# Splitting the staged row tiles into thirds for a one-block convolution, with loads six units ahead

## The chip, the core and the metric

The kernel runs on one core of a Trainium2 chip. The metric is the device time of one execution in microseconds (us). Before the change three runs took 3682.8, 3675.8 and 3668.18 us; their median, 3675.8 us, is the time before. The profiled execution spans 3665.1 us from its first to its last instruction.

Names used below: PE is TensorE (PEld its weight loads), ACT is ScalarE, DVE is VectorE, POOL is GpSimd, SP is SyncE, whose queue (SPq in the profile) issues most of the DMAs.

## What is computed

Input x has shape (2, 256, 64, 64): B = 2 images, C = 256 channels, 64 rows of 64 pixels, all in float32. Layer 0 is full attention over the 4096 pixels of an image with 8 heads, then a 1x1 convolution and a blend with a mask. Layer 1 gates the channels, runs attention in 8x8 windows, adds that to its input, shuffles the channels in four groups, and ends with two grouped 7x7 convolutions whose sigmoid gates the result. The change concerns this last part, in the reference:

```python
x = x + o
g = 4
x = x.reshape(b, g, c // g, h, w).transpose(0, 2, 1, 3, 4).reshape(b, c, h, w)
y = lax.conv_general_dilated(x, sa_w1, (1, 1), [(3, 3), (3, 3)], feature_group_count=cr)  # 256 -> 64
y = relu(_bn(y + sa_b1, bn1...))
y = lax.conv_general_dilated(y, sa_w2, (1, 1), [(3, 3), (3, 3)], feature_group_count=cr)  # 64 -> 256
y = _bn(y + sa_b2, bn2...)
return x * sigmoid(y)
```

## The kernel before

**Main loop.** The function `pipeline` walks 1024 slots (image b, chunk c of 512 queries, group g of four heads, block m of 128 keys), in an order written out by hand (`tc.manual_schedule()`): the instructions of each engine run in the order in which the Python code emits them. Each slot has score matmuls on PE (L483), exponentials on ACT (L491), value products on PE (L505) and sums for the softmax denominators on DVE (L507). Beside these slots, `stage(b, c)` does what remains of layer 0 and the window attention of layer 1 for one chunk of eight image rows. Its last step writes the eight rows of `xo` to the DRAM scratch `x_s[b]` (L734, L739, the names xo and xs in the profile).

**The convolutions.** `convolve(b, blocks)` is a generator that is advanced a step at a time between slots. The 64 image rows are cut into three row blocks, `BLOCKS = ((0, 0, 24), (17, 24, 40), (34, 40, 64))`: first row loaded, first and last row of the result; 30 rows are loaded for each. The image b = 0 is convolved in one pass over all three blocks. The image b = 1 is convolved in two passes: blocks 0 and 1 as soon as chunk 5 is staged, and block 2 alone, `convolve(1, (2,))`, after the last chunk, when the attention slots are over and nothing else is left to run.

A pass works through `NU = 8` units of 32 channels (eight groups of four). For a unit u:

- `load_w(u)` (L760 to L764) loads the band matrices of both convolutions, w1 and w2, 896 KB each, from DRAM, into a pool of four buffers that both share (`wsp`).
- `load_x(u)` (L766 to L772) loads the unit's image rows from `x_s[b]`: for each row block four DMAs of 30 rows x 8 channels x 70 pixels, 65.6 KB. The destination is one of two fixed tiles `xcs[0]` and `xcs[1]`, each with room for three row blocks: `[P, len(BLOCKS), UG, WP]`.
- `conv1(u)` runs the first convolution as 112 matmuls (L782) from w1 and the x tile, and ACT writes the rectified result into `yc` (L790).
- `conv2(u)` runs the second as 112 matmuls (L803) from w2 and `yc` into two PSUM tiles; ACT turns these into the gate z by a tanh (L813) and a scale (L819).
- `gate(u, z)` multiplies z by the x tile on DVE (L825) and POOL issues the output DMAs (L832), four for each row block.

The x tile of a unit is thus read twice, by conv1 and, at the unit's very end, by gate.

**The order of a pass.** First load_w(0) and load_w(1); then load_x(0) and load_x(1); then conv1(0); and for each u: conv1(u+1), conv2(u), gate(u), then load_w(u+2) and load_x(u+2). PE therefore runs conv1(0), conv1(1), conv2(0), conv1(2), conv2(1), conv1(3) and so on, ending with conv2(6), conv2(7). SP issues in the same order: the two weight DMAs of a unit, then its row DMAs. A DMA whose buffer is not free, or whose source is not written yet, holds up the whole SP queue behind it. For the last pass, load_w(0) and load_w(1) are emitted early, at the start of the last stage (the list `ahead`). In the built program a weight DMA of unit u in the last pass waits for these readers of its buffer: w1 of unit u for conv2(u-3), w2 of unit u for conv1(u-1); for u = 2, w1 waits for conv1(0) and w2 for conv1(1). The DMAs of SP also use eight completion counters in turn, so each waits for the landing of the one eight places before it.

Of the kernel before, what the change touches and what calls it, by code (L numbers as in the profile page):

```python
# [17 lines left out]
B, C, H, W = 2, 256, 64, 64  # L18
# [16 lines left out]
KS, PAD = 7, 3  # L35
# [5 lines left out]
BLOCKS = ((0, 0, 24), (17, 24, 40), (34, 40, 64))  # L41
NG = C // 4
UG = 8
NU = NG // UG
# [8 lines left out]
def conv_seq_kernel(ctx: ExitStack, tc: tile.TileContext, a, out):  # L53
# [6 lines left out]
    def psum2(name):  # L60
        return ps.tile([P, 2, CH], F32, tag="s", name=name)
# [18 lines left out]
    xcs, ycs = [], []  # L80
# [41 lines left out]
    with (  # L122
# [19 lines left out]
        for b in range(B):  # L142
            src = a["x"][b].rearrange("(k p) h w -> p k (h w)", p=P)
            for c in range(NCHUNK):
                x = x0.tile([P, KC, CH], F32, tag="x", name=f"x0_{b}_{c}")
# [220 lines left out]
    for kc in range(KC):  # L366
        d = wf[:, kc, kc * P : (kc + 1) * P]
# [7 lines left out]
    def pipeline(arm, shifted, pools):  # L375
# [191 lines left out]
        def stage(b, c):  # L567
            x, f = xts.pop((b, c)), fts.pop((b, c))
            if (b, c) == (B - 1, NCHUNK - 1):

                assert not convs
                ahead.append(convolve(b, conv_after[b, c]))
                next(ahead[0])
# [171 lines left out]
            if (b, c) in conv_after:  # L745
                convs.append(ahead.pop(0) if ahead else convolve(b, conv_after[b, c]))
# [7 lines left out]
        def convolve(b, blocks):  # L754
            nb = len(blocks)
            xs, w1s, w2s, ys = {}, {}, {}, {}
            dst = out[b].rearrange("(g i) r w -> i r g w", i=4)
            tag = f"{arm}_{b}_{blocks[0]}"

            def load_w(u):  # L760
                for ws, d, i in ((w1s, w1_s, 1), (w2s, w2_s, 2)):
                    t = wsp.tile([P, 32, UW], F32, tag="w", name=f"w{i}{tag}_{u}")
                    nc.sync.dma_start(t, d[u])
                    ws[u] = t  # L764

            def load_x(u):  # L766
                x = xs[u] = xcs[u % 2]
                for n, blk in enumerate(blocks):
                    r = BLOCKS[blk][0]
                    for q in range(4):  # L770
                        gs = slice(NG * q + UG * u, NG * q + UG * u + UG)
                        nc.sync.dma_start(x[4 + q : 4 + 4 * RB : 4, n], x_s[b][r : r + RB, gs, :])  # L772

            def conv1(u):
                if u >= NU:
                    return
                x, w = xs[u], w1s.pop(u).rearrange("p m (g d) -> p g d m", g=UG)
                s = psum2(f"c1{tag}_{u}")
                for q in range(2):
                    for d in range(KS):  # L780
                        for j in range(4):
                            nc.tensor.matmul(  # L782
                                s[32 * j : 32 * j + 32, q, 0 : nb * W],
                                w[:, 4 * q + j, d, :],
                                x[:, 0:nb, 4 * q + j, d : d + W],
                                start=(d == 0),
                                stop=(d == KS - 1),
                            )
                y = ys[u] = ycs[u % 2]
                nc.scalar.activation(  # L790
                    y[:, :, 0:nb, PAD : PAD + W],
                    s[:, :, 0 : nb * W].rearrange("p q (n x) -> p q n x", n=nb),
                    AF.Relu,
                )

            def conv2(u):
                y, w = ys.pop(u), w2s.pop(u).rearrange("p m (i q d) -> p q d (m i)", q=2, i=4)
                tiles = [psum2(f"c2{tag}_{u}_{hh}") for hh in range(2)]
                for q in range(2):
                    for d in range(KS):  # L800
                        for j in range(4):
                            r = slice(32 * j, 32 * j + 32)
                            nc.tensor.matmul(  # L803
                                tiles[j // 2][:, j % 2, q * nb * W : (q + 1) * nb * W],
                                w[r, q, d],
                                y[r, q, 0:nb, d : d + W],
                                start=(d == 0),
                                stop=(d == KS - 1),
                            )
                z = cp.tile([P, 2, 4, len(BLOCKS) * W], F32, tag="z", name=f"z{tag}_{u}")  # L810
                z = z[:, :, :, 0 : nb * W]
                for hh in range(2):
                    nc.scalar.activation(  # L813
                        z[:, :, 2 * hh : 2 * hh + 2, :],
                        tiles[hh][:, :, 0 : 2 * nb * W].rearrange("p j (q f) -> p q j f", q=2),
                        AF.Tanh,
                        scale=0.5,
                    )
                nc.scalar.activation(z, z, AF.Copy, bias=0.5, scale=0.5)  # L819
                return z  # L820

            def gate(u, z):
                x = xs.pop(u)
                z = z.rearrange("p q j (n x) -> p (q j) n x", n=nb)
                nc.vector.tensor_mul(  # L825
                    z, z, x[:, 0:nb, :, PAD : PAD + W].rearrange("p n g x -> p g n x")
                )
                for n, blk in enumerate(blocks):
                    x0, r0, r1 = BLOCKS[blk]
                    for i in range(4):  # L830
                        p0, p1 = (4 * (r + 1 - x0) + i for r in (r0, r1))
                        nc.gpsimd.dma_start(  # L832
                            dst[i, r0:r1, UG * u : UG * u + UG, :], z[p0 : p1 - 3 : 4, :, n, :]
                        )

            load_w(0)
            load_w(1)
            yield
            load_x(0)
            load_x(1)  # L840
            yield
            conv1(0)
            yield
            for u in range(NU):
                conv1(u + 1)
                yield
                z = conv2(u)
                yield
                gate(u, z)
                if u + 2 < NU:  # L850
                    load_w(u + 2)
                    load_x(u + 2)
                yield

        def run_convs():
# [134 lines left out]
```

## Time and profile before

| What | Before |
|---|---|
| median time (three runs) | 3675.8 us |
| span of the profiled execution | 3665.1 us |
| PE busy over the span | 3382.0 us (92%) |
| DVE busy | 2718.2 us (74%) |
| ACT busy | 2328.0 us (64%) |
| last attention product (L505) ends | about 3454 us |
| last write of rows to x_s issued | 3520.37 us |
| last pass: first conv1 matmul | 3528.71 us |
| last pass: last conv2 matmul ends | 3655.28 us |
| last output DMAs issued | 3657.37 us to 3659.81 us |

Up to about 3454 us the attention slots keep PE, ACT and DVE busy together. From there to 3520 us the last stage runs alone, and then the last convolution pass alone. So the profile has to be read for that stretch by itself: the busy shares of the whole span say nothing of it. In the views used below, the chain of waits gives for each step its start, its length and what it was; the timeline gives for each merged row the start, the length, the engine, the line, the operation, and in brackets the idle time of the engine before it and what ended it; the view of stretches gives the busy time of each engine in each stretch with the granted TensorE clock (1.00 is full speed), the share in which the DMA engines were busy, and the bytes moved.

### The profile page before, as it was taken

What the parts mean: (1) busy time and instruction counts of PE and PEld (TensorE: products, weight loads), DVE (VectorE), ACT (ScalarE), POOL (GpSimd) and SP (SyncE); (2) the same over time, 40 slices, a digit from 0 to 9 for tenths busy, and PEclk for the clock granted to TensorE, in tenths of its full rate; (3) what the DMA queues carried; (4) which work ended last, traced back from release to release, by engine and by line L of the source; (5) the groups of instructions that cost most, each with busy time, mean ns of one, the idle gap of its engine ahead of it and who ended that gap; (6) DMA issues with size and microseconds to landing.
All of it is one profiled execution on the core that took longest, in us unless ns stands there. A gap on an engine that the chain in (4) does not pass through costs nothing.

```text
span 3665.1 us, 60054 instructions
## 1 busy us (share of the span) xinstructions
PE 3382.0 (92%) x25482; PEld 1223.8 (33%) x25482; DVE 2718.2 (74%) x1767; ACT 2328.0 (64%) x2549; POOL 231.4 (6%) x377
## 2 busy tenths in 40 slices
PE   9999999999999999999999899999999999779865
PEld 3432222222222222222234443323232323445345
DVE  3229989898989898989895565798989898545710
ACT  2238777777777777777775555677777777435510
POOL 5400000000000000000001111000000000011001
PEclk9999999999999999999999999999999999889965
DMA  8642112121212121112232232121212121332222
GB/s 311 191 132 64 52 52 59 51 60 50 62 47 62 49 62 50 53 56 55 61 114 90 86 108 79 50 62 51 61 49 60 49 61 50 117 116 88 69 79 92
DMA packets 139880, 284.86 MB, mean 78 GB/s; under 512 B 31560, under 2 KB 34012, under 8 KB 139600
## 3 DMA queue, kind: packets, MB, share of 16 engines
q1 hardware_dynamic: 120032, 242.60, 21.4%
q0 software_dynamic: 15760, 35.80, 3.6%
q8 instruction: 203, 3.33, 0.4%
q10 hardware_dynamic: 3808, 2.50, 0.2%
q14 instruction: 77, 0.63, 0.1%
HBM read 223.17 MB, written 60.65 MB: 77 GB/s over the span
## 4 chain that ended last, share of the span: by engine, by line
PE 41%; issue 27%; DVE 16%; ACT 3%; SPq 3%; DMA 3%; POOL 0%; DVEq 0%; ACTq 0%; POOLq 0%
PE sa L483 15%; PE ava L505 12%; DVE suma L507 11%; PE c2a L803 5%; PE c1a L782 3%; SPq L772 3%; PE qka L632 2%; ACT ea L491 2%; DMA xc<-xs 1%; DVE rda L528 1%; PE vwa L649 1%; PE opa L724 1%; DVE za L825 1%; PE hya L583 1%; PE ca1a L606 1%
## 5 line engine op out<-in xcount | busy, mean ns | idle before, releaser
L507 DVE TENSOR_TENSOR suma<-suma,ea 128x2048 f32<-128x2048 f32 x960 | 2199.7, 2291 | 448.9 <-ACT ea L491 371.2
L491 ACT ACTIVATE ea<-sa 128x1024 f32<-128x1024 f32 x2048 | 1984.5, 1023 | 428.7 <-PE sa L483 292.5
L483 PE MATMUL sa<-qa,ka 32*128 32x512 f32 x8192 | 1350.5, 650 | 72.6 <-ACT ea L491 40.3
L505 PE MATMUL ava<-ea,va 128*32 128x512 f32 x8192 | 1110.0, 614 | 0.0
L483 PEld LDWEIGHTS sa<-qa,ka 32*128 32x128 f32 x8192 | 436.0, 185 | 923.0 <-issue 479.6
L505 PEld LDWEIGHTS ava<-ea,va 128*32 128x32 f32 x8192 | 162.3, 108 | 795.7 <-issue 793.3
L782 PE MATMUL c1a<-xc,w1a 128*32 128x192 f32 (+2 forms) x2688 | 106.8, 336 | 124.6 <-DMA xc<-xs 124.6
L739 POOL DMA_DIRECT2D xs<-xo x32 | 28.4, 892 | 2397.4 <-DVE xo L734 2396.9
L803 PE MATMUL c2a<-yc,w2a 32*128 32x192 f32 (+2 forms) x2688 | 172.3, 415 | 1.0 <-issue 1.0
L803 PEld LDWEIGHTS c2a<-yc,w2a 32*128 32x128 f32 x2688 | 167.2, 336 | 15.6 <-issue 13.6
L832 POOL DMA_DIRECT2D out_dram<-za x192 | 112.5, 594 | 750.5 <-ACT ea L491 501.9
L632 PE MATMUL qka<-ua,qkv_w 128*128 128x512 f32 x256 | 128.5, 625 | 28.7 <-ACT qka L640 25.0
L782 PEld LDWEIGHTS c1a<-xc,w1a 128*32 128x32 f32 x2688 | 97.6, 156 | 143.1 <-issue 135.5
L790 ACT ACTIVATE yc<-c1a 128x384 f32<-128x384 f32 (+2 forms) x24 | 9.3, 388 | 208.1 <-PE c1a L782 208.1
L825 DVE TENSOR_TENSOR za<-za,xc 128x1536 f32<-128x1536 f32 (+2 forms) x24 | 29.3, 1222 | 131.5 <-ACT za L819 131.5
L813 ACT ACTIVATE za<-c2a 128x768 f32<-128x768 f32 (+2 forms) x48 | 26.3, 594 | 155.2 <-PE c2a L803 155.1
L640 ACT ACTIVATE qka<-qka,qkv_b 128x512 f32<-128x512 f32 x64 | 44.0, 687 | 107.7 <-PE qka L632 106.5
L528 DVE RECIPROCAL rda<-rda 128x512 f32<-128x512 f32 x32 | 107.1, 3346 | 2.8 <-ACT rda L525 2.8
L507 DVE TENSOR_TENSOR suma<-ea,ea 128x2048 f32<-128x2048 f32 x32 | 73.1, 2284 | 19.0 <-DMA ka<-ks 14.0
L632 PEld LDWEIGHTS qka<-ua,qkv_w 128*128 128x128 f32 x256 | 43.9, 191 | 113.5 <-issue 56.8
L724 PE MATMUL opa<-ota,out_w 128*128 128x512 f32 x128 | 65.3, 633 | 13.3 <-ACT ya L731 12.4
L166 DVE TENSOR_SCALAR qst<-q,bq 128x512 f32<-128x512 f32 x32 | 24.0, 751 | 69.3 <-PE q L155 45.0
(124 smaller groups left out, 1633.3 us busy)
## 6 DMA issues: line engine op xcount, KB each, us to landing
ka<-ks SPq DMA_DIRECT2D x256, 256.0 KB, 2.6
va<-vs SPq DMA_DIRECT2D x256, 256.0 KB, 2.6
w1a<-w1s SPq DMA_DIRECT2D x24, 896.0 KB, 4.7
w2a<-w2s SPq DMA_DIRECT2D x24, 896.0 KB, 6.6
xc<-xs SPq DMA_DIRECT2D x192, 65.6 KB, 2.5
xs<-xo POOLq DMA_DIRECT2D x32, 280.0 KB, 6.7
x<-in_x_dram SPq DMA_DIRECT2D x16, 512.0 KB, 4.9
ks<-kst SPq DMA_DIRECT2D x32, 256.0 KB, 2.5
```

Of the source, the lines that this page charges most:

```text
L483: nc.tensor.matmul(o, k[r, cols], q[r, g, :], start=True, stop=not shifted)
L491: nc.scalar.activation(e[:, 2 * hh : 2 * hh + 2, :], tiles[hh], AF.Exp, scale=SCALE0)
L505: nc.tensor.matmul(av[r, :], v[:, m % PB, r], e[:, j, :], start=start, stop=stop)
L507: nc.vector.tensor_add(total, first[0] if m == 1 else total, e)
L528: nc.vector.reciprocal(rd, rd)
L632: nc.tensor.matmul(s[:, j, :], wqkv[:, kc, o : o + P], u[:, kc, :], start=(kc == 0), stop=(kc == KC - 1),)
L724: nc.tensor.matmul(s[:, oc, :], wo[:, kc, oc * P : (oc + 1) * P], ot[:, kc, :], start=(kc == 0), stop=(kc == KC - 1),)
L772: nc.sync.dma_start(x[4 + q : 4 + 4 * RB : 4, n], x_s[b][r : r + RB, gs, :])
L782: nc.tensor.matmul(s[32 * j : 32 * j + 32, q, 0 : nb * W], w[:, 4 * q + j, d, :], x[:, 0:nb, 4 * q + j, d : d + W], start=(d == 0), stop=( ...
L803: nc.tensor.matmul(tiles[j // 2][:, j % 2, q * nb * W : (q + 1) * nb * W], w[r, q, d], y[r, q, 0:nb, d : d + W], start=(d == 0), stop=(d = ...
L825: nc.vector.tensor_mul(z, z, x[:, 0:nb, :, PAD : PAD + W].rearrange("p n g x -> p g n x"))
L832: nc.gpsimd.dma_start(dst[i, r0:r1, UG * u : UG * u + UG, :], z[p0 : p1 - 3 : 4, :, n, :])
```

## The change

A pass over nb row blocks now cuts each of the two x tiles into `len(BLOCKS) // nb` parts of nb row blocks, and unit u uses tile u % 2 and, within it, part u // 2 modulo the number of parts. For nb = 3 and nb = 2 there is one part, and everything is as before. For nb = 1, the last pass, there are three parts in each tile, so that six units have places of their own. `depth` is the number of places: 2 for the first two passes, 6 for the last. The rows of the first `depth` units are loaded before conv1(0), and after gate(u) the rows of unit u + depth go into the place that gate(u) has just read. It is meant to take the row loads off the path from one unit's gate to the next conv1. No instruction is added or removed; 24 row DMAs now stand together at the start of the last pass, where eight stood, and only those of units 6 and 7 are left between the weight DMAs.

```diff
             def load_x(u):
-                x = xs[u] = xcs[u % 2]
+                if u >= NU:
+                    return
+                n = u // 2 % (len(BLOCKS) // nb) * nb
+                x = xs[u] = xcs[u % 2][:, n : n + nb]
                 for n, blk in enumerate(blocks):
...
                             nc.tensor.matmul(
                                 s[32 * j : 32 * j + 32, q, 0 : nb * W],
                                 w[:, 4 * q + j, d, :],
-                                x[:, 0:nb, 4 * q + j, d : d + W],
+                                x[:, :, 4 * q + j, d : d + W],
...
                 nc.vector.tensor_mul(
-                    z, z, x[:, 0:nb, :, PAD : PAD + W].rearrange("p n g x -> p g n x")
+                    z, z, x[:, :, :, PAD : PAD + W].rearrange("p n g x -> p g n x")
                 )
...
             load_w(0)
             load_w(1)
             yield
-            load_x(0)
-            load_x(1)
+
+            depth = 2 * (len(BLOCKS) // nb)
+            for u in range(depth):
+                load_x(u)
             yield
             conv1(0)
...
                 gate(u, z)
                 if u + 2 < NU:
                     load_w(u + 2)
-                    load_x(u + 2)
+                load_x(u + depth)
                 yield
```

## The prediction

> **What bounds the kernel now.** The page first: PE is busy 92% of the span, yet its groups of instructions name one wait that has nothing to do with attention.
>
> ```profile
> L782 PE MATMUL c1a<-xc,w1a 128*32 128x192 f32 (+2 forms) x2688 | 106.8, 336 | 124.6 <-DMA xc<-xs 124.6
> L803 PE MATMUL c2a<-yc,w2a 32*128 32x192 f32 (+2 forms) x2688 | 172.3, 415 | 1.0 <-issue 1.0
> ```
>
> PE stood idle 124.6 us before first-convolution matmuls, always until rows had landed. The change touches only the last pass, so the next view is the waits of the stretch 3522 to 3665 us (us in total, times, longest):
>
> ```profile
> PE c1a L782 <- DMA xc<-xs: 53.7, 8, 10.1
> SPq L772 <- DVE za L825: 53.8, 6, 10.1
> ```
>
> The first line has eight waits; units 0 and 1 account for 10.09 and 0.51 us (their rows can't be read before the last stage has written them). The second says why the other six come late: SP holds the row loads of a unit until DVE has gated the unit two before. The chain of waits gives one such round whole (start, length, what):
>
> ```profile
> 3561.77 0.71 DVE za L825
> 3562.48 0.02 issue
> 3562.49 0.81 SPq L772
> 3563.31 0.05 issue
> 3563.36 0.77 SPq L772
> 3564.12 0.04 issue
> 3564.17 0.76 SPq L772
> 3564.93 0.04 issue
> 3564.97 2.42 DMA xc<-xs
> 3567.39 0.14 issue
> 3567.53 3.08 PE c1a L782 x112
> 3570.61 7.03 PE c2a L803 x112
> ```
>
> Gate, four DMA issues one after the other, a landing, conv1, conv2, and again. From the start of one conv1 to the next are 17.4 us, of which PE works 10.25. The idle times before conv1(2) to conv1(7) in the timeline are 6.90, 7.14, 7.53, 7.25, 7.13 and 7.19: together 43.1 us. That is all that the change can take.
>
> **How long the two convolutions take without the wait.** The view of stretches shows conv1(1), conv2 of a middle unit, and the end, where conv2(6) and conv2(7) stand together (PE, PEld, DVE, ACT, POOL busy; granted clock; DMA share; GB/s):
>
> ```profile
> 3532.00:3534.50 2.50, 2.06 (x116) 2.02 (x116) 0.00 (x0) 0.27 (x1) 0.00 (x0) 0.84 0.58 166
> 3623.30:3630.30 7.00, 6.98 (x112) 6.79 (x112) 0.00 (x0) 0.28 (x1) 0.00 (x0) 0.50 0.40 133
> 3640.70:3648.00 7.30, 7.30 (x116) 7.30 (x116) 0.00 (x0) 0.53 (x2) 0.00 (x0) 0.73 0.01 2
> 3648.00:3655.30 7.30, 7.26 (x110) 6.89 (x108) 0.69 (x1) 1.42 (x4) 2.44 (x4) 0.50 0.14 33
> ```
>
> conv2 takes 7.0 us at clock 0.50 and at 0.73: its weight loads, 6.79 us of 7.00, pace it. conv1 does depend on the clock: 2.08 us for conv1(1), warm behind conv1(0), and 3.22 at 0.50.
>
> **What the Trainium skill says.** "TensorE: Matmul & The Clock Gate", Part 1: the array runs at half clock until it has been busy through a free-running window of some 3.4 us, and falls back after an idle one. The trace agrees on the two levels, and goes further: between 3646 and 3655 us PE works without a break, in conv2 alone, and the clock is 0.50 all the same. So conv2 does not keep it up. The same page, "LDWEIGHTS", says that a weight load costs by its columns, not by its rows; conv2's loads (32 rows x 128 columns) take 6.90 us for 112 where conv1's (128 x 32) take 3.01, which agrees in direction. "DMA: Bandwidth & Descriptors", "Issuing engines are not separate DMA queues": all queues share 16 engines. And "Queues, rings and completion order" there: in a ring descriptors are taken in order, so rows issued behind weights wait for these. The trace has it for image 0, where the longest row landing is 10.3 us against a median of 2.4, at a DMA share near 1.
>
> **The change part by part.**
>
> *The row loads of units 2 to 5 go ahead: six waits on gates become two.* The built program shows no wait of their own on them but the landing of the eighth DMA before. At 0.81 us an issue, eight issues are 6.5 us, and a row landing is 2.5: no stall. Gone are the gaps before conv1(2) to conv1(5) as far as rows made them. Units 6 and 7 still wait for gate(0) and gate(1), but have 30 us and more before they are used: nothing.
>
> *What moves on SP.* In the trace the eighth row issue begins at 3529.52 and ends near 3530.3. Sixteen more at 0.81 take 13.0 us, to 3543.3. The weights of unit 2 stand behind them; w1 went out at 3531.99 before and now goes at 3543.3. Queued behind it on SP are w2(2), rows 6, w1(3); on PE conv1(2) and everything after wait for w1(2). It lands after 4.6 us (median of six w1 loads here), plus 0.15 to the first matmul: conv1(2) starts at S = 3548.05, where before it was 3550.15. So the first gap does not vanish; it shrinks by only 2.1 us, and its cause is now a weight load. A bound from the other side: in image 0's pass 24 row issues took 24.16 us, 1.0 each, under crowded DMA; at that rate S is 3551.2, a loss of 1.0 instead.
>
> *Units 3 to 7.* PE then runs conv1 3.22 and conv2 7.03, 10.25 a unit, if weights keep up:
> - w1(3) is free after conv2(0), issued behind rows 6 at about 3548.4, landed 3553.0; needed at S + 10.25 = 3558.3.
> - w2(3) waits for conv1(2), 3551.3; landed by 3556, needed much later.
> - Rows 7 wait for gate(1), which ends 2.1 us after conv2(1), at 3560.4; four issues to 3563.7; then w1(4), landed at 3568.3. Needed at S + 20.5 = 3568.55. Just in time; with 5.0, the longest landing here, 0.2 us late.
> - From then on no rows stand in the way: w1(u) goes when conv2(u-3) ends and has 10.25 us for 4.6. w2(u) goes when conv1(u-1) ends, some 20 us ahead.
>
> Five units at 10.25 are 51.25; from conv1(7) on the trace has 3637.47 to 3655.28, 17.81. I add 0.3 for w1(4) and seams: PE ends at 3548.05 + 51.25 + 17.81 + 0.3 = 3617.4, against 3655.28. The gain is 37.9 us: 2.1 from the first gap, 36.2 from the other five, less the 0.3. The tail behind conv2(7) stays.
>
> *The rest costs nothing.* Slices of the tiles change addresses, not instructions; the other two passes have one part and the same order. ACT, DVE and POOL work 1.57, 0.69 and 2.44 us a unit and lie beside 10.25 of PE. PSUM and the z buffers come free as before, behind a conv1 of 3.2 us. DMA bytes a unit: 1.84 MB of weights, 0.2 of output, in 10.25 us 198 GB/s; the trace shows 359 GB/s at full share in 3534.5 to 3537.1. There PE also lost 1.02 us inside conv2(0), while two weight loads stood together. That may recur where w1(4) and w2(4) follow each other; the trace doesn't show what it was, so I price it at nought to one us, take nought, and keep the rest for the range.
>
> **Rivals.**
> - *The clock rises.* Without gaps conv1 might run at 2.08: six times 1.14 is 6.8 less, 3631. Against it: the clock falls during conv2, as shown, and a conv2 stands before each of these conv1s.
> - *Weights take the place of rows in every unit.* If each w1 went out only as the PE became free for it, the gap would be 4.75 in place of 7.2: 5 x 2.45 + 2.1 = 14.4 saved, 3661. Against it: the buffers' waits as listed give w1 ten us of lead.
> - *DMA as the bound, slower than before.* If the DMA gave no more than the stretch's mean of 107 GB/s, 2.04 MB a unit would take 19.1 us, 1.65 more than now: five units 8.2, and 1.0 for the late S: 3685. For it: 24.16 us for 24 issues, a sign of crowding; against it: 359 GB/s moved in this same stretch.
>
> **How the numbers follow.** 3675.8 - 37.9 = 3637.9, rounded to 3638: chance 0.80. The clock 0.10, weights 0.06, DMA 0.04. The low end takes in the clock's 3631 and 6 for the spread of the runs before (3668.18 to 3682.8): 3625. The high end takes S at 3551.2 (+3.1), five stalls of 1 us, 0.5 more for w1(4) and 5.4 for that spread: 3652. Left out are weights and DMA, 0.10. Over 0.5% is 18.4 us: the first two cases are faster, 0.90; weights fall within 0.5%, with DMA mostly, 0.08; slower by more 0.02.
>
> **What would show it.** Right: after conv1(2), first-convolution matmuls without idle time on rows; conv1 starts 10.25 apart; one gap of about 5 us before conv1(2), ended by w1; SP issuing 24 row DMAs to about 3543; conv2(7) ending near 3617; clock 0.50 at each conv1. Wrong: a gap before every conv1 that ends with w1a; conv1 at 2.1 us; matmuls stretched or broken while weights move; rows landing late behind weights; another time before 3522.

## The result, and the profile after

The changed kernel takes 3633.02 us (median of four runs, 3626.75 to 3640.51) against 3671.99 us of the kernel before (four runs, 3665.8 to 3682.8): ratio 0.9892, 95% interval 0.9859 to 0.9924. Forecast were 3638 us within 3625 to 3652, and faster. Direction, size and place of the gain came as forecast; one term, the gap before conv1(2), did not. With four runs each, the interval allows a gain of about 28 to 52 us.

The page's two groups of the convolutions, which answer to those shown of before (L782 has become L785, L803 has become L806):

```profile
L785 PE MATMUL c1a<-xc,w1a 128*32 128x192 f32 (+2 forms) x2688 | 110.1, 342 | 92.3 <-DMA xc<-xs 73.5
L806 PE MATMUL c2a<-yc,w2a 32*128 32x192 f32 (+2 forms) x2688 | 172.1, 412 | 0.0
```

The idle time before first-convolution matmuls fell from 124.6 to 92.3 us, 32.3 less. The waits of the stretch from 3500 us to the end (us in total, times, longest) show what is left in the last pass:

```profile
PE c1a L785 <- DMA xc<-xs: 10.7, 2, 10.2
PE c1a L785 <- issue: 8.2, 2, 7.8
```

Rows are waited for twice, by units 0 and 1, as before. The other six waits of PE on rows are gone. In their place stand two that the profile puts down to nothing ("issue"). The SP queue's own waits say what SP was doing:

```profile
SPq L763 <- PE c2a L806: 17.0, 3, 6.8
SPq L763 <- PE c1a L785: 11.9, 4, 3.3
SPq L775 <- DVE za L828: 8.7, 1, 8.7
```

53.8 us in six waits of row loads on the gate have become 8.7 in one (rows 7 on gate(1)). The weight loads now wait for their buffers in good time. The chain of waits, from gate(0) to the start of conv1(4) (start, length, what):

```profile
3541.94 0.64 ACT za L822
3542.58 6.75 issue
3549.34 3.22 PE c1a L785 x112
3552.56 7.02 PE c2a L806 x111
3559.58 3.15 PE c1a L785 x112
3562.73 7.02 PE c2a L806 x110
3569.75 0.36 issue
3570.11 3.22 PE c1a L785 x112
```

Before the change a gate, four issues and a landing stood between one conv2 and the next conv1. Now conv1(3) follows conv2(1) at once, and so do all later ones but conv1(4), which is 0.36 us late. Only the gap before conv1(2) is still there. SP's timeline tells its cause (start, length, what):

```profile
3521.56 22.46 SPq L775 DMA_DIRECT2D xc<-xs  x24
3544.12 0.49 SPq L763 DMA_DIRECT2D w1a<-w1s  x1
3544.72 0.38 SPq L763 DMA_DIRECT2D w2a<-w2s  x1
```

w1(2) leaves SP behind 24 row issues and lands 5.1 us later, at 3549.2; conv1(2) starts at 3549.34. Last, the stretches that hold conv1(1), a conv2 in the middle, conv2(6) and conv2(7) (PE, PEld, DVE, ACT, POOL busy; clock; DMA share; GB/s):

```profile
3531.90:3534.20 2.30, 2.29 (x116) 2.23 (x116) 0.00 (x0) 0.00 (x0) 0.00 (x0) 0.82 0.40 86
3583.60:3590.60 7.00, 7.00 (x116) 6.90 (x112) 0.00 (x0) 0.28 (x1) 1.73 (x3) 0.74 0.61 208
3604.00:3611.30 7.30, 7.30 (x118) 7.30 (x116) 0.00 (x0) 0.52 (x2) 1.69 (x3) 0.73 0.12 29
3611.30:3618.60 7.30, 7.28 (x110) 6.91 (x110) 0.69 (x1) 1.43 (x4) 2.44 (x4) 0.50 0.15 33
```

conv2 keeps its 7.0 us with the DMA at 208 GB/s beside it, half as much again as the 133 of before.

**A length that can be compared.** The runs of one kernel spread over 14 us and more (up to 28 us in the experiments below), and the traces show where: the second write of rows to xs, which opens the last pass, is issued anywhere from 3515.93 to 3531.17 us, in a part of the program that the edits below leave as it is. So the experiments are read by the length of the last pass, from the issue of that second write to the end of conv2(7). Before it is 3520.37 to 3655.28, 134.9 us; after, 3519.74 to 3618.58, 98.8 us: 36.1 us less, by itself nearly the whole difference of the medians (39.0).

### The profile page after: what moved, and what is told of

Its sections match the earlier page's. It is cut to its first block, busy times and chain, and to the rows that moved or that the text cites. A ratio compares the mean times of both kernels' runs of the same rounds, so it can differ in the third digit from the quotient of the medians.

```text
span 3628.9 us, 60051 instructions
## 1 busy us (share of the span) xinstructions
PE 3372.7 (93%) x25482; PEld 1225.3 (34%) x25482; DVE 2718.9 (75%) x1767; ACT 2326.7 (64%) x2549; POOL 231.4 (6%) x377
## 3 DMA queue, kind: packets, MB, share of 16 engines
q8 instruction: 203, 3.33, 0.4%
## 5 line engine op out<-in xcount | busy, mean ns | idle before, releaser
L785 PE MATMUL c1a<-xc,w1a 128*32 128x192 f32 (+2 forms) x2688 | 110.1, 342 | 92.3 <-DMA xc<-xs 73.5
L806 PE MATMUL c2a<-yc,w2a 32*128 32x192 f32 (+2 forms) x2688 | 172.1, 412 | 0.0
L806 PEld LDWEIGHTS c2a<-yc,w2a 32*128 32x128 f32 x2688 | 167.1, 336 | 14.6 <-issue 12.7
L785 PEld LDWEIGHTS c1a<-xc,w1a 128*32 128x32 f32 x2688 | 99.4, 157 | 111.9 <-issue 101.5
## 6 DMA issues: line engine op xcount, KB each, us to landing
xc<-xs SPq DMA_DIRECT2D x192, 65.6 KB, 2.6
```

The source lines that it names most:

```text
L785: nc.tensor.matmul(s[32 * j : 32 * j + 32, q, 0 : nb * W], w[:, 4 * q + j, d, :], x[:, :, 4 * q + j, d : d + W], start=(d == 0), stop=(d = ...
L806: nc.tensor.matmul(tiles[j // 2][:, j % 2, q * nb * W : (q + 1) * nb * W], w[r, q, d], y[r, q, 0:nb, d : d + W], start=(d == 0), stop=(d = ...
```

## Experiments

Each kernel starts from the changed one. The table gives the length of the last pass and the idle time of PE in it from conv2(0) on. A gap stands before a convolution, and the number in brackets is that of the conv1 that waited; a break stands inside one. Each ratio is to runs of the kernel before made beside it.

| Kernel | Last pass, us | Idle, us | Median, us | Ratio to before (95%) |
|---|---|---|---|---|
| before | 134.9 | 43.1 in six gaps, break of 1.02 | 3672.0 | 1 |
| the change | 98.8 | gap (2) 7.84, (4) 0.36 | 3633.0 | 0.9892 (0.9859 to 0.9924) |
| the change again | 99.9 | gap (2) 9.23, (4) 0.73 | 3631.2 | 0.9899 (0.9874 to 0.9924) |
| own places, two ahead | 94.4 | gap (4) 1.48, (6) 0.94, (7) 0.40, break of 0.28 | 3638.3 | 0.9911 (0.9892 to 0.9930) |
| four ahead | 93.2 | gap (2) 3.25 | 3635.6 | 0.9901 (0.9882 to 0.9919) |
| weights of unit 2 first | 95.7 | gap (3) 4.00, break of 1.23 | 3630.4 | 0.9896 (0.9872 to 0.9919) |
| extra traffic | 103.7 | gap (2) 9.43, (4) 3.56, break of 0.66 | 3646.4 | 0.9921 (0.9898 to 0.9944) |
| three ahead | 90.6 | break of 1.20 | 3629.8 | 0.9894 (0.9867 to 0.9922) |
| three ahead again | 89.4 | none | 3625.4, one run | |
| pairs | 93.6 | breaks of 0.18, 1.40, 1.76 | 3625.7 | 0.9876 (0.9852 to 0.9901) |
| pairs again | 93.3 | breaks of 1.04, 0.89, 1.49 | 3622.2, one run | |
| pairs, weights left out | 88.4 | break of 0.45 | 3621.5, one run | |

The intervals of the ratios overlap: between the changed kernels only the last pass can be told apart, and it repeats within 1.2 us where it was taken twice (the change, three ahead, pairs).

### How far the last pass repeats

The changed kernel once more, with no edit, on the chip on which three ahead and the pairs first ran:

> The change itself once more, on the chip of the two runs beside it, for a direct comparison and as a measure of how far the length of the last pass repeats: 98.9 us from the second write of xs to the end of conv2(7), within 1 us if differences of 2 us between kernels are to be read; the gap before conv1(2) 7 to 9 us, that before conv1(4) below 1 us.

PE's timeline, conv1(2) and conv1(4):

```profile
3547.19 3.22 PE L785 MATMUL c1a<-xc,w1a 128*32 128x64 f32 x112 [9.23 <-issue]
...
3568.34 3.22 PE L785 MATMUL c1a<-xc,w1a 128*32 128x64 f32 x112 [0.73 <-ACT za L816]
```

The same two gaps, 1.4 and 0.4 us longer, and a last pass of 99.9 us against 98.8. Differences of some 2 us between the last passes of two kernels can therefore be read; smaller ones, as between two ahead and four ahead below, can not.

### Is it the place or the look-ahead?

```diff
-            depth = 2 * (len(BLOCKS) // nb)
+            depth = 2
```

> Edit: the thirds stay, but the rows are loaded two units ahead in the old order (rows 0 and 1 first, rows u+2 after gate(u) and behind the weights of u+2). Theory A, the wait was for the place that the gate still read: rows u+2 now wait only for SP to reach them, which is when w2(u+2) has gone out at the end of conv1(u+1). From there 0.35 + three issues of 0.81 + a landing of 2.7 = 5.5 us, or up to 7.8 if they ride behind w2, against 7.03 of conv2(u): gaps before conv1(2) to conv1(7) of 0 to 0.9 us, and w1(2) goes at 3532 again, so that the first gap is gone as well. PE would end 5 to 8 us before that of the change: 3625 to 3628 us, ratio to before 0.987 to 0.988. Theory B, it is the six units of look-ahead that matter, because rows are slow behind weights: gaps of 3 us or more before every conv1, 3648 us or more, ratio 0.993 or more.

PE's timeline in this kernel, the first convolutions of units 2 to 7 (the bracket is idle time before it):

```profile
3546.41 3.22 PE L785 MATMUL c1a<-xc,w1a 128*32 128x64 f32 x112
...
3556.71 3.22 PE L785 MATMUL c1a<-xc,w1a 128*32 128x64 f32 x112
...
3568.42 3.22 PE L785 MATMUL c1a<-xc,w1a 128*32 128x64 f32 x112 [1.48 <-ACT za L822]
...
3578.60 3.22 PE L785 MATMUL c1a<-xc,w1a 128*32 128x64 f32 x112
...
3589.78 3.04 PE L785 MATMUL c1a<-xc,w1a 128*32 128x64 f32 x112 [0.94 <-DMA xc<-xs]
...
3600.24 2.95 PE L785 MATMUL c1a<-xc,w1a 128*32 128x64 f32 x112 [0.40 <-DMA xc<-xs]
```

Three gaps of 2.8 us together are left of 43.1, with the row loads in the very order and as few units ahead as before. So the wait was for the place, theory A. Look-ahead adds little: rows that follow their own w2 through the queue land after up to 7.5 us, which is the odd microsecond late. That holds for the gap of 1.48 too, which is longer than the 0.9 allowed for: the profile names ACT, but the last rows of unit 4 land at 3568.3, just before conv1(4) starts. And the first gap is gone, because w1(2) is again the ninth DMA of the pass and not the twenty-fifth. The last pass is 4.4 us shorter than with six ahead, as theory A had it (5 to 8). The whole time does not show that. Its median, 3638.3, misses the 3625 to 3628 expected, and its interval (0.9892 to 0.9930) can't be told from that of the change: the runs are spread as said, and in the profiled one the pass began 3.6 us later than in that of the change.

### The first gap: how many row issues stand before w1(2)

```diff
-            depth = 2 * (len(BLOCKS) // nb)
+            depth = 2 if nb > 1 else 4
```

> Edit: rows of four units in place of six before the first conv1 of the last pass, then four ahead. Theory A, the gap before conv1(2) is w1(2) standing behind row issues on SP: eight issues fewer are 6.5 us, w1(2) goes at about 3537.5, lands by 3542.5, the gap falls from 7.8 to 1.0 to 1.5 us, and the 0.36 us before conv1(4) is gone, since no rows wait for a gate: about 3626 us, ratio 0.9875. Theory B, w1(2) is slow because weights and rows share the DMA engines: the gap stays above 5 us, 3631 to 3633 us.

SP, and conv1(2) on PE, in this kernel's timelines:

```profile
3545.36 0.50 SPq L763 DMA_DIRECT2D w1a<-w1s  x1
3545.96 1.09 SPq L763 DMA_DIRECT2D w2a<-w2s  x1
```

```profile
3553.01 3.22 PE L785 MATMUL c1a<-xc,w1a 128*32 128x64 f32 x112 [3.25 <-issue]
```

The eight issues fewer bring w1(2) forward from 24.4 to 16.9 us after the second write, 7.5 us, a little over the 6.5 expected. The gap before conv1(4) is gone too, since rows 6 and 7 no longer wait for a gate. But w1(2) landed after 7.6 us, 2.5 more than in the first trace of the change, so that 3.25 us of the gap are left in place of the 1.0 to 1.5 expected. The queue position, theory A, is the larger part. Theory B would put the long landing down to sharing: between 3544 and 3554 us the core's DMA moved 2.49 MB at 249 GB/s, of which w1(2) is 0.92. That is not shown. w2(2) goes out 0.6 us behind w1(2) here, but it does so in the two traces of the change and in the one with extra traffic as well, where w1(2) landed after 5.1, 6.2 and 4.7 us.

The other way to bring w1(2) forward is to let the weights of unit 2 go before the rows of units 2 to 5:

```diff
-            for u in range(depth):
+            for u in range(2):
                 load_x(u)
...
                 conv1(u + 1)
+                if u == 0 and nb == 1:
+                    load_w(2)
+                    for n in range(2, depth):
+                        load_x(n)
                 yield
...
-                if u + 2 < NU:
+                if u + 2 < NU and (u > 0 or nb > 1):
                     load_w(u + 2)
```

> Edit: six places and the loads six ahead, but the weights of unit 2 go out before the rows of units 2 to 5. Theory A: w1(2) goes at 3531.5, w2(2) at 3534.2, both land before conv2(0) ends at 3541.2; rows 2 behind them land by about 3541. The gap of 7.8 us before conv1(2) goes to 0 to 1 us, the 0.36 us before conv1(4) stays: 3625 to 3626 us, ratio 0.987. Theory B, rows and weights in the DMA engines are the limit: rows 2 come late instead, the gap is 3 us or more and the time 3628 us or more.

The first gap went, as theory A expected, but another came that neither theory named. On PE:

```profile
3540.65 3.22 PE L785 MATMUL c1a<-xc,w1a 128*32 128x64 f32 x112
3543.80 7.09 PE L806 MATMUL c2a<-yc,w2a 32*128 32x64 f32 x112
3554.89 3.22 PE L785 MATMUL c1a<-xc,w1a 128*32 128x64 f32 x112 [4.00 <-issue]
```

and on SP:

```profile
3532.21 17.41 SPq L775 DMA_DIRECT2D xc<-xs  x20
3549.72 0.49 SPq L763 DMA_DIRECT2D w1a<-w1s  x1
```

The twenty row issues, 17.4 us, now stand in front of w1(3). It lands 5.1 us after 3549.72 and conv1(3) starts at once. The burst of row issues has to be paid by whichever weights come next. Moved by one unit, it costs 4.0 us in place of 7.8: counted from the second write, w1(3) leaves 7.6 us later than w1(2) did in the change, but PE is ready for it 11.4 us later.

### Is the DMA near its bound?

```diff
+    w3_s = dram.tile([NU, P, 32, UW], F32, name="w3s")
...
                 conv1(u + 1)
+                if nb == 1 and u + 2 < NU:
+                    nc.scalar.dma_start(w3_s[u], w1_s[u])
                 yield
```

> Edit: the change, and beside it ACT issues one copy of a 917 KB weight block from DRAM to DRAM for each of units 2 to 7 (bytes that nothing reads), half as much again as the weights of a unit. Theory A, PE bounds the last pass and the DMA has room: w1(2) and w1(4) land 1 to 3 us later, the other units are unmoved at 10.2 us: 3634 to 3638 us, ratio 0.990 to 0.991. Theory B, the DMA is about to become the bound: a gap of 3 us or more before each conv1, 3651 us or more, ratio 0.994 or more.

```profile
3561.53 3.22 PE L786 MATMUL c1a<-xc,w1a 128*32 128x64 f32 x112 [9.43 <-issue]
...
3585.50 3.22 PE L786 MATMUL c1a<-xc,w1a 128*32 128x64 f32 x112 [3.56 <-DMA w1a<-w1s]
```

```profile
3573.88 5.81 SPq L776 DMA_DIRECT2D xc<-xs  x4
```

Half as much again of weight traffic lengthens the pass by 4.9 us over the first trace of the change and by 3.8 over the second. What is clear of their spread is one place: conv1(4), which waits 3.56 us against 0.36 and 0.73. Most of that is SP: the four issues of rows 7, which stand before w1(4), took 5.81 us, where they took 3.50 and 3.64 in the change. conv1(2) started 30.4 us after the second write, against 29.6 and 30.5 in the change, so the longer gap before it is not shown to come from the traffic. Units 3, 5, 6 and 7 follow without a gap; there is a break of 0.66 us inside conv1(7). So theory B, a gap of 3 us or more before each conv1, is out. The whole time, 3646.4, lies above the 3634 to 3638 that theory A gave; in the profiled run the pass began 11.4 us later than with the change, which is the larger part of it.

### The shortest pass

```diff
-            depth = 2 * (len(BLOCKS) // nb)
+            depth = 2 if nb > 1 else 3
```

> Edit: the thirds stay; rows of three units before the first conv1, then three ahead. Theory A, two queues have to be served at once: rows need only their own place and a unit of lead, and weights must not stand behind many row issues. w1(2) then goes 3.2 us later than with two units ahead, 3.5 us before it would be late; rows are landed before their conv1: no gap above 0.5 us before conv1(2) to conv1(7). From the second write of xs to the end of conv2(7) 91 to 92 us, against 98.9 for the change, 94.4 with two ahead and 93.2 with four. About 7 us below the change: ratio to before 0.987 to 0.989. Theory B, two weight loads together starve whatever else is loading: gaps of 1 us or more remain, 93 us or more.

> Three ahead once more, for a second trace of the shortest pass: 90 to 92 us from the second write of xs to the end of conv2(7), no gap ended by rows or by w1 above 0.5 us; a break of about 1 us inside a convolution may or may not come again.

The first trace has no gap ended by rows or weights, but a break inside conv1(2):

```profile
3536.96 1.72 PE L785 MATMUL c1a<-xc,w1a 128*32 128x64 f32 x52
3539.88 1.93 PE L785 MATMUL c1a<-xc,w1a 128*32 128x64 f32 x60 [1.20 <-issue]
```

The second has not even that:

```profile
3545.53 2.81 PE L785 MATMUL c1a<-xc,w1a 128*32 128x64 f32 x112
3548.27 7.09 PE L806 MATMUL c2a<-yc,w2a 32*128 32x64 f32 x112
3555.29 3.00 PE L785 MATMUL c1a<-xc,w1a 128*32 128x64 f32 x112
3558.22 7.09 PE L806 MATMUL c2a<-yc,w2a 32*128 32x64 f32 x112
```

90.6 and 89.4 us: 8 us or more below the change, with one number altered, and below two ahead (94.4) and four ahead (93.2). Rows have a unit of lead, and w1(2) stands behind four extra row issues. Its margin is smaller than the 3.5 us expected: it landed less than 0.2 us before conv1(2) in the first trace (after 7.8 us) and 2.1 in the second (after 5.9). The pass is a little shorter than the 91 to 92 us expected, in part because some conv1s take less than 3.22 us (more on this below, under the clock). For the whole, its ratio of 0.9894 cannot be told from that of the change beside it (0.9899).

### Is conv1 slow because the clock is low?

Here the pass takes its units in pairs; the core of the edit (the load of a unit's weights is split into one for w1 and one for w2):

```diff
+                for u in range(0, NU, 2):
+                    conv1(u)
+                    conv1(u + 1)
+                    load_w1(u + 2)
+                    load_w1(u + 3)
+                    load_x(u + 2)
+                    load_x(u + 3)
+                    yield
+                    for v in (u, u + 1):
+                        z = conv2(v)
+                        gate(v, z)
+                        load_w2(v + 2)
+                        yield
```

> Edit: the thirds stay; the last pass takes units in pairs (conv1 of two units, then conv2 of both), rows and w1 of the next pair loaded behind the conv1s, w2 behind each conv2. Theory A, the clock is at half speed when a conv1 follows a conv2 and full for a conv1 that follows a conv1: the second conv1 of a pair takes 2.0 to 2.1 us, the first 3.2; each conv2 that follows a conv2 loses 0.5 us to the tanh before it, as conv2(7) does now. Three pairs save 3 x (1.2 - 0.5) = 2 us over a pass without gaps: 89 to 90 us from the second write of xs to the end of conv2(7). Theory B, conv1 is cold for another reason: 3.2 us each, and the pass is 92 to 93 us.

```profile
3550.84 5.29 PE L785 MATMUL c1a<-xc,w1a 128*32 128x64 f32 x195
3557.53 0.72 PE L785 MATMUL c1a<-xc,w1a 128*32 128x64 f32 x29 [1.40 <-issue]
...
3572.74 5.08 PE L785 MATMUL c1a<-xc,w1a 128*32 128x64 f32 x224
```

The undisturbed pair takes 5.08 us where two single conv1s take 6.44. The stretches of its first and second conv1 show why (the columns as above; the clock is the third number from the end):

```profile
3572.74:3575.90 3.16, 3.16 (x122) 3.16 (x124) 0.69 (x1) 1.07 (x3) 0.97 (x2) 0.50 0.59 200
3575.90:3577.70 1.80, 1.80 (x116) 1.79 (x108) 0.00 (x0) 0.28 (x1) 1.47 (x3) 0.93 0.97 271
```

The first runs at 0.50, the second at 0.93: theory A of the clock. But the pass, 93.6 us, missed the 89 to 90 expected, for the most part because conv1 broke off twice, 3.2 us together. Two more runs asked whether the weight traffic does that:

> Edit: the pairs of the run before, but the weights of units 2 to 7 of the last pass are left out: those units use the weights of units 0 and 1. Theory A, the breaks inside conv1 (1.40 and 1.76 us in the run before, 1.20 in the one with three ahead) come with heavy weight traffic: no break is left, and the last pass is 89 to 90 us from the second write of xs, which the pairs were expected to give. Theory B, they belong to the order of the instructions: breaks of more than 1 us stay, and the pass is 92 us or more.

> The pairs once more, for a second trace: under theory A the breaks come again where weights move, not always in the same places, 2 to 4 us in all, and the pass is 92 to 95 us; under theory B they stand in the same places, 1.4 and 1.8 us inside conv1(3) and conv1(7).

Without weights:

```profile
3549.94 4.55 PE L785 MATMUL c1a<-xc,w1a 128*32 128x64 f32 x195
3554.94 0.72 PE L785 MATMUL c1a<-xc,w1a 128*32 128x64 f32 x29 [0.45 <-issue]
...
3570.16 5.06 PE L785 MATMUL c1a<-xc,w1a 128*32 128x64 f32 x224
```

The pairs again:

```profile
3546.47 5.43 PE L785 MATMUL c1a<-xc,w1a 128*32 128x64 f32 x195
3552.78 0.72 PE L785 MATMUL c1a<-xc,w1a 128*32 128x64 f32 x29 [0.89 <-issue]
```

Both theories were half right. A break stands at the same instruction in all three traces, behind the 195th of 224 matmuls, as theory B had it. It is longer with the traffic, 1.40 and 0.89 us with weights, 0.45 without, and the break of 1.76 and 1.49 us in the last pair is absent without weights: that is theory A's part, on a single trace without weights. The pass without weights is 88.4 us, a little under the 89 to 90 that the pairs were to give; with weights it is 93.3 to 93.6, so that the pairs as built are no gain over three units ahead.

## Why the prediction was right, and where it was not

*What bounds the last pass.* Right. The six waits on rows are gone, and the run with own places alone shows by itself that the reuse of the place was their cause.

*Units 3 to 7.* Right. From the start of conv1(2) to the end of conv2(7) the sum was 51.25 + 17.81 + 0.3 = 69.36 us; the two traces of the change have 69.24 and 69.46. w1(4), "just in time", is 0.36 and 0.73 us late, its landing 4.7 and 5.0.

*The first gap.* Here a term was mis-sized: "conv1(2) starts at S = 3548.05, where before it was 3550.15". Counted from the second write of xs, S was forecast at 27.7 us, stood at 29.8 before, and came at 29.6 and 30.5. So the step that was to save 2.1 us saved 0.2 and lost 0.7. Two things made it up. Sixteen more row issues took 14.3 us in the first trace, 0.90 each, not 0.81, because three of them held SP for 1.1 to 1.4 us: w1(2) left 24.4 us after the second write and not 22.9. And it landed after 5.1 and 6.2 us, not 4.6. The 4.6 was read from six loads of before, behind each of which w2 went out 2.6 us later or more; now it follows within 0.7. In the five traces where it does, w1(2) landed after 4.7, 5.1, 6.2, 7.6 and 7.8 us, and w1(4) of the change, followed as closely, after 4.7 and 5.0. So the close follower alone does not make a landing long; what does stays open. The gap itself was to be about 5 us and is 7.84: 1.9 of that is S, and 1.1 is that PE is done with conv2(0) earlier, for the most part because the break of 1.02 us there did not come again. The wider bound given, S at 3551.2 or 30.8 from the write, holds both traces. But its 1.0 us an issue was no pace: the 24.16 us of image 0 have one wait of 3.0 us in them, between the fifth and the sixth issue.

*The gain.* 37.9 us were forecast for the last pass; it gave 36.1 and 35.0. The difference is S. That the median nevertheless fell by 39.0, more than forecast, is luck: it lies within the spread of the part before the pass.

*The clock.* Right for the change: each conv1 behind a conv2 takes 3.22 us, and the pairs confirm the reason that was given against this rival. But the rival is not worth nothing everywhere. With three ahead, where no gap is left, the clock rises while conv1 still runs: conv1(2) to conv1(6) of the second trace take 2.81, 3.00, 3.12, 3.21 and 3.22 us, and the mean clock over conv1(2) is 0.62.

*The DMA and weight rivals.* Ruled out as the bound: with 2.9 MB a unit in place of 2.0, only conv1(4) starts later beyond the spread, by some 3 us. What the prediction had not asked is whether six units ahead were needed at all. They were not, and with the burst of row issues that they bring the pass is 8 us or more longer than with three.

## What to carry to other kernels

When a load waits for the buffer of work that has not ended, first ask whether another place for it is enough. Here that alone, in the old order, took away 40.3 of 43.1 us of gaps. A deeper look-ahead on the same in-order queue puts its issues in front of whatever comes next; count issues times the cost of one, and find the first load behind them that someone waits for. And take a landing time that was read from a load with the queue to itself as the lower end: w1(2) took 4.7 to 7.8 us here where 4.6 had been read.

## What had not been expected

**PE breaks off at fixed places, each time shortly after an instruction packet.** In eight traces PE stops inside a convolution, twelve times in all, for 0.2 to 1.8 us, and the profile names no wait. Before the change this is the 1.02 us inside conv2(0), behind its 37th matmul. With three ahead it is behind the 52nd of conv1(2), 75 + 52 = 127 matmuls on. With the pairs it is behind the 37th of conv2(0), then 75 + 112 + 195 = 382 on, three times 127.3, then 29 + 224 + 224 + 224 + 188 = 889 on, seven times 127.0. With extra traffic it is behind the 77th of conv1(7), 75 + 10 x 112 + 77 = 1272 on from the same place, ten times 127.2.

The page counts 203 packets of 3.33 MB on the instruction queue, 16.4 KB each, for the whole program. The packets of this queue in the traces fit the stops in time and in number. Each of the twelve stops ends 1.2 to 1.6 us after such a packet has ended (in the pairs, for one, a packet runs from 3555.11 to 3556.06 us, and PE goes on at 3557.53). And over the 1, 3, 7 and 10 times 127 matmuls named above, the queue brings 1, 3, 7 and 10 packets. So PE seems to run out of instructions at the edge of a packet when the next one comes late. No run altered the instructions or their packets alone, so this is not shown by experiment.

**A row DMA holds its queue longer than a weight DMA does.** In the change a row issue (30 rows of 560 elements, 65.6 KB) holds SP for 0.76 us in the median, a weight issue of 896 KB for 0.32 to 0.50. So the time of the burst that delayed w1(2) goes with the number of row DMAs rather than with their bytes.
